# Second feed-forward's chunks in pairs by seven products, unread products at a norm, and the last additions shared out, in a four-layer attention kernel

## The chip, the cores and the metric

The kernel runs on one core of a Trainium2 chip, in float32, from one launch. The metric is the time of the whole launch in microseconds (us); the time of a kernel is the median of its runs. One further execution is taken by the hardware profiler, and all rows of a profile and a trace are of that one. The core's engines have short names in the profile: PE (matrix products), PEld (PE's weight loads, which lie beside the products), DVE (vector), ACT (scalar, with the transcendental functions), POOL (GpSimd) and SP (issues DMAs). L277 is line 277 of the kernel.

## The reference

512 tokens (2 batches of 256) of width 256 pass four layers. Each has a cross-attention to a context of 2 x 512 rows and a feed-forward, both on a layer norm of `x` and added to `x` with a gate:

```python
x = x + jnp.tanh(g_xattn[0]) * _L0_xattn_ref(_layernorm(x), ctx_2048)
x = x + jnp.tanh(g_ffn[0]) * _L0_ffn_ref(_layernorm(x), L0_ffn_W_up, L0_ffn_W_gate, L0_ffn_W_down)
x = x + jnp.tanh(g_xattn[1]) * _L1_xattn_ref(_layernorm(x), ctx_2048, Wq, Wk, Wv, Wo)
x = x + jnp.tanh(g_ffn[1]) * _L1_ffn_ref(_layernorm(x), L1_ffn_w_gate_up, L1_ffn_w_down)
x = x + jnp.tanh(g_xattn[2]) * _L2_xattn_ref(_layernorm(x), ctx_2048, Wq, Wg, bg, Wkv, Wo)
x = x + jnp.tanh(g_ffn[2]) * _L2_ffn_ref(_layernorm(x), router_w, gate_w, up_w, down_w)
x = x + jnp.tanh(g_xattn[3]) * _L3_xattn_ref(_layernorm(x), ctx_2048, mask_BxS2_bk0)
x = x + jnp.tanh(g_ffn[3]) * _L3_ffn_ref(_layernorm(x), router, w_up_gate, w_down, shared_w_up_gate, shared_w_down)
```

The change touches three places of it. The second feed-forward is dense, 256 to 1024 and back:

```python
gate_up = jnp.einsum('bsh,oh->bso', h_shard, w_gate_up)    # 256 -> 2 x 1024
gate, up = jnp.split(gate_up, 2, axis=-1)
h = jax.nn.silu(gate) * up
out = jnp.einsum('bsi,hi->bsh', h, w_down)                 # 1024 -> 256
```

The fourth attention has no weights: softmax of `x` against the context's rows, under a mask, and the same rows as values. The fourth feed-forward takes each token through the two best of eight small experts, `y = sum of w[k] * out_buf[expert k, place k]`, and through one shared expert; both are added.

## The kernel before, in words

**Tiles.** `x` stays in SBUF as four tiles of 128 tokens x 256 (`x[:, n, :]`, NT = 4). A norm takes, for each tile, `bn_stats` and `bn_aggr` on DVE (L217, L218), two POOL instructions for `rstd` (L219 adds epsilon, L220 takes the power -1/2), and one DVE instruction for `xn` (L236, `norm_apply`). Two PE transposes of each tile into PSUM (tag `tr`) and an ACT copy give `xT`, width on the partitions, laid out as batch, half of the width, 256 tokens. Most products with `x` take `xT` as the moving side, 256 columns (one batch) or 512 (both), with two products to a sum, one for each half of the width.

**Who orders the work.** The program is written as one text; for each engine the order of the text is its order, apart from what `inline` does. `inline(i, line)` chains an instruction behind the last one given to the same list: `line` for DVE, `pool_line` for POOL, `pe_line` for PE. Where a list is empty (after `clear()`) no such chain is made and a planner may move the instruction; `None` appended starts a chain anew. `chain` (L277) is the helper that issues nearly all products, so they have one line in the profile; `add_to_x` (L280) is the helper of all additions to `x`, `x = acc * scalar + x` in one DVE instruction. Buffers come from rotating pools: `q4` (4 KB per partition), `q2`, `q1` in SBUF; `ps_mm` (`mm`), `ps_tr` (`tr`, `mm_t`) and `ps_acc` (`acc`) in PSUM. A tile is given out when the earlier user of its buffer is through.

**The second attention**, in front of the first place, has 16 heads of 128. `l1_attend` ends each half head with a reciprocal and a multiplication on DVE and two additions on POOL (`all_t` L840, `all_r` L841), which keep sums for a check of the range. Its keys, queries and values are made in pairs of heads by seven products of blocks: `weight_sums` (L593 on) forms four sums of weight blocks on POOL (L597 to L600), `batch_sums` (L585 on) four sums of the blocks of `xT` (L588 to L591), and `seven_queries` (L651 on) issues seven products of 256 columns and builds four output blocks of 128x256 from them by one ACT copy and four DVE additions (L672, L675, L676, L679). The eight products that the plain way takes are 2 x 2 x 2: two blocks of output columns, two batches, two halves of the width to be summed.

**The second feed-forward** is `dense_ffn`, called once with `whole_keys2` as `between`. Its three weights are `aw`, `lw` (256 x 1024 each) and `dw`. `hidden` (L300 on) goes through eight chunks of 128 columns of the 1024. Chunks 0 and 1 go batch by batch, four products of 256 columns for each batch, and stand between the transposes of the norm and the keys of the third attention (`whole_keys2`, eight tiles of context; `k` is L956), which fill PE while the norm is made. Chunks 2 to 7 take four products of 512 columns each, two for `aw`, two for `lw`; then ACT takes the silu from PSUM and DVE multiplies by the other (L317) into `hT`. `down` then takes one tile of tokens after the other: eight products of 256 columns into `acc`, and `add_to_x`. Behind it comes the third attention's norm. POOL's two DMAs that clear the tables `xg` and `yg` in DRAM, and `iota` and `zero`, stand in the text around it; `k2` and `v2` hold the third attention's keys and values.

**The third feed-forward's end and the fourth attention's norm.** `l2_back` (L1362) puts the experts' rows back to their tokens by products into `y`; `l3_stats` adds `y` to `x` and takes the norm's statistics, `norm_apply` makes `xn`, and `l3_turned(n)` transposes it (L1423). `l3_scores` then takes products of 128 columns against the context into `ps3`, and `l3_exps` the exponentials on ACT.

**The end.** `yg` in DRAM holds each token's two rows; four DMAs gather them to `rows[n]` (`o3g`, L1718 on), two on SP's queue and two on ACT's. `shared_down(n)` gives the shared expert's `accs`. `final(n)` adds a tile's two rows, each times its weight `kept`, by two `add_to_x`; the `accs` take one more. `store(n)` sends the tile out on SP's queue.

Of the kernel before, what the change touches and what calls it, by code (L numbers as in the profile page):

```python
# [17 lines left out]
F32 = mybir.dt.float32  # L18
# [3 lines left out]
AF = mybir.ActivationFunctionType  # L22
# [3 lines left out]
P = 128  # L26
NT = 4
D = 256
T = NT * P
B = 2  # L30
# [19 lines left out]
def flamingo(ctx: ExitStack, tc: tile.TileContext, a: dict, out: bass.AP):  # L50
# [122 lines left out]
    def gf(layer):  # L173
        return tg[:, 4 + layer : 5 + layer]
# [60 lines left out]
    def norm_apply(n, xn, stats):  # L235
        inline(nc.vector.tensor_scalar(xn[:, n, :], x[:, n, :], *stats, ALU.subtract, ALU.mult))  # L236
# [35 lines left out]
    def mm(shape=None):  # L272
        return ps_mm.tile(shape or [P, 512], F32, tag="mm", name="mm")
# [5 lines left out]
    def add_to_x(n, acc, scalar, cols=slice(0, D)):  # L279
        return inline(nc.vector.scalar_tensor_tensor(x[:, n, cols], acc, scalar, x[:, n, cols], ALU.mult, ALU.add))  # L280
# [11 lines left out]
    def load_table(fn, last, why):  # L292

        t = small.tile([P, 1], F32, tag="warm", name="warm", bufs=1)
        behind(nc.scalar.activation(t, eps_ln, fn), last, why)

    def hidden(xT, chunks, act_w, lin_w, hT, both_w=None, pause=lambda ci, b: False):


        ps = {}  # L300
        for ci, (off, sz), ts in by_batch(chunks):
            if sz == 64:
                p = mm()
                chain(p, [(both_w(k), batch(xT, k)) for k in range(2)])
                s = q2.tile([P, T], F32, tag="q2", name="silu")
                nc.scalar.activation(s[64:], p[:64], AF.Silu)
                nc.vector.tensor_mul(hT[ci // 2][64:, ci % 2, :], s[64:], p[64:])
                continue
            if ci not in ps:
                ps[ci] = mm(), mm()  # L310
            pa, pb = ps[ci]
            for w, p in ((act_w, pa), (lin_w, pb)):
                chain(p[:sz, ts], [(w(k, off, sz), batch(xT, k, ts)) for k in range(2)])
            if ts.stop == T:
                s = q2.tile([P, T], F32, tag="q2", name="silu")
                silus[:] = [nc.scalar.activation(s[:sz, :], pa[:sz, :], AF.Silu)]
                nc.vector.tensor_mul(hT[ci // 2][:sz, ci % 2, :], s[:sz, :], pb[:sz, :])  # L317
            if pause(ci, ts.stop // T):
                yield
# [4 lines left out]
    def down(hT, chunks, w, scalar, tiles=range(NT)):  # L324

        for n in tiles:
            acc = ps_acc.tile([P, D], F32, tag="acc", name="acc")
            chain(acc, [(hT[ci // 2][hidden_rows(sz), ci % 2, n * P : (n + 1) * P], w(ci, hidden_rows(sz)))
                        for ci, (_, sz) in enumerate(chunks)])
            add_to_x(n, acc, scalar(n))  # L330
# [262 lines left out]
    def weight_sums(pool, tag, u, v):  # L593

        cols = u.shape[2]
        t = pool.tile([P, 4, cols], F32, tag=tag, name="wsum")
        nc.gpsimd.tensor_add(t[:, 0, :], v[:, 0, :], v[:, 1, :])  # L597
        nc.gpsimd.tensor_sub(t[:, 1, :], t[:, 0, :], u[:, 0, :])
        nc.gpsimd.tensor_sub(t[:, 2, :], u[:, 0, :], v[:, 0, :])
        nc.gpsimd.tensor_sub(t[:, 3, :], u[:, 1, :], t[:, 1, :])  # L600
        return t
# [33 lines left out]
    def seven_keys(p):  # L635
# [8 lines left out]
        def product(dst, w, t):  # L644
# [3 lines left out]
                     context_of(slice(0, M)), product, lambda t: t,  # L648
                     [[t[:, b * M : (b + 1) * M] for b in range(B)] for t in kT])

    def seven_queries(p):  # L651

        w = l1_w[p // 2][0]
        u, v = (w[:, :, (2 * p + i) % 4 * HD : ((2 * p + i) % 4 + 1) * HD] for i in range(2))
        s = weight_sums(q2, "q2", u, v)
        yield
        qT = q4.tile([P, 4, 256], F32, tag="q4", name="qT")
        queries1.append(qT)

        def two(tr, *of):  # L660
            t = ps_tr.tile([P, 2, 256], F32, tag="tr", name="mm_t") if tr else mm([P, 2, 256])
            for i, (w, b) in enumerate(of):
                nc.tensor.matmul(t[:, i, :], lhsT=w, rhs=b, start=True, stop=True)  # L663
            return t

        def both(i):
            return qT[:, i : i + 1, :].to_broadcast([P, 2, 256])

        m1 = two(True, (u[:, 0, :], xT[:, 0, 0, :]))
        nc.scalar.copy(qT[:, 1, :], m1[:, 0, :])  # L670
        m26 = two(False, (u[:, 1, :], xT[:, 0, 1, :]), (s[:, 1, :], x_sums[:, 1, :]))
        nc.vector.tensor_add(qT[:, 0:4:3, :], both(1), m26)  # L672
        yield
        m57 = two(True, (s[:, 0, :], x_sums[:, 0, :]), (s[:, 2, :], x_sums[:, 2, :]))
        nc.vector.tensor_add(qT[:, 1:3, :], both(3), m57)  # L675
        nc.vector.tensor_add(qT[:, 3, :], qT[:, 2, :], m57[:, 0, :])  # L676
        yield
        m34 = two(False, (s[:, 3, :], xT[:, 1, 1, :]), (v[:, 1, :], x_sums[:, 3, :]))
        nc.vector.tensor_add(qT[:, 1:3, :], qT[:, 1:3, :], m34)  # L679
        yield  # L680

    def seven_values(g):

# [23 lines left out]
    def dense_ffn(layer, act, lin, dn, between):  # L707

        aw = act.rearrange("p (k e) -> p k e", k=2)
        lw = lin.rearrange("p (k e) -> p k e", k=2)  # L710
        dw = dn.rearrange("p (c d) -> p c d", d=D)
        pe_line.append(None)
        xn = q4.tile([P, NT, D], F32, tag="q4", name="xn")
        xT = q4.tile([P, B, 2, 256], F32, tag="q4", name="xT")
        hT = [q4.tile([P, 2, T], F32, tag="q4", name="hT") for _ in range(4)]
        chunks = hidden(xT, FCH, lambda k, o, s: aw[:, k, o : o + s], lambda k, o, s: lw[:, k, o : o + s], hT,
                        pause=lambda ci, b: ci < 2)
        for n in range(NT):
            norm_apply(n, xn, norm_stats(n))
            tr = ps_tr.tile([P, 2, P], F32, tag="tr", name="tr")  # L720
            for k in range(2):
                inline(nc.tensor.transpose(tr[:, k, :], xn[:, n, k * P : (k + 1) * P], ident), pe_line)
            nc.scalar.copy(tokens(xT, n), tr)
            if n == 1:
                between(0)
            if n == 2:
                next(chunks)
                between(1)
        for _ in range(3):
            next(chunks)  # L730
        pe_line.clear()
        for _ in chunks:
            pass
        down(hT, FCH, lambda c, s: dw[:, c, :], lambda n: gf(layer))

    def ternary_ffn():

# [204 lines left out]

    half_bg = small.tile([P, 2], F32, tag="half_bg", name="half_bg", bufs=1)
    behind(nc.gpsimd.tensor_scalar_mul(half_bg, bg, 0.5), l0_pool, "its data come late")
    k2 = [q4.tile([P, 4, D], F32, tag="q4", name="k2") for _ in range(B)]
    v2 = [q4.tile([P, 3, 2, P + 1], F32, tag="q4", name="v2") for _ in range(3)]
    for t in v2:
        nc.gpsimd.memset(t[:, :, :, P : P + 1], 1.0)
    def negatives(z):
        t = q2.tile(list(z.shape), F32, tag="q2", name="fm")  # L950
        inline(nc.vector.tensor_scalar_min(t, z, 0.0))
# [34 lines left out]


    load_table(AF.Exp, silus[0], "the table of exponentials with tanh")
    kv = q2.tile([P, B, 2, P], F32, tag="q2", name="kv")
    ks = small.tile([P, B, 2, 8], F32, tag="ks2", name="ks2", bufs=1)  # L990
    for t in (line, pe_line):
# [378 lines left out]
    for q in range(QUADS + 2):  # L1370
# [15 lines left out]
            hTs[q] = l2_turn(h)  # L1386
        if q >= 2:
            l2_back(q - 2, os.pop(q - 2), backs.pop(q - 2), y)
    pe_line.clear()
    shd = slab[:, 0, 0 : 6 * D].rearrange("p (c d) -> p c d", d=D)  # L1390
    nc.gpsimd.memset(shd[0:64, 5, :], 0.0)
    nc.sync.dma_start(shd[:, 0:5, :], a["l3_shd"][0 : 5 * P, :].rearrange("(c p) d -> p c d", p=P))
# [13 lines left out]
    nc.vector.reduce_sum(none, p, axis=AX.X)  # L1406
    nc.vector.tensor_scalar(none, none, 0.0, None, ALU.is_le)

    for t in (line, pe_line):
        t.append(None)  # L1410
    xn = q4.tile([P, NT, D], F32, tag="q4", name="xn")
    xT = q4.tile([P, B, 2, 256], F32, tag="q4", name="xT")
    ctxT_rows3 = ctxT.rearrange("p b k (h i r) -> p b k h i r", h=2, r=2)
# [6 lines left out]
    def l3_turned(n):  # L1420
        tr = ps_tr.tile([P, 2, P], F32, tag="tr", name="tr")
        for k in range(2):
            inline(nc.tensor.transpose(tr[:, k, :], xn[:, n, k * P : (k + 1) * P], ident), pe_line)  # L1423
        nc.scalar.copy(tokens(xT, n), tr)
# [44 lines left out]
    l3_stats(3)  # L1469
    norm_apply(2, xn, stats3[2])  # L1470
    norm_apply(3, xn, stats3[3])
    l3_turned(0)
    l3_scores(0, ps3[0], slice(0, P), [0])
    l3_turned(1)
# [140 lines left out]
    def shared_down(n):  # L1615
        acc = ps_acc.tile([P, D], F32, tag="acc", name="acc")
        chain(acc, [(hS[c // 2][:, c % 2, n * P : (n + 1) * P], shd[:, c, :]) for c in range(6)])
        return acc
# [104 lines left out]
    def final(n):  # L1723
        for k in range(2):
            add_to_x(n, rows[n][:, k, :], kept[:, k, n : n + 1])

    def store(n):
        nc.sync.dma_start(out[n * P : (n + 1) * P, :], x[:, n, :])

    for n in range(2):  # L1730
        add_to_x(n, accs[n], gf(3))
    accs = [shared_down(n) for n in (2, 3)]
    final(0)
    store(0)
    add_to_x(2, accs[0], gf(3))
    for n in (1, 2):
        final(n)
        store(n)
    final(3)
    add_to_x(3, accs[1], gf(3))  # L1740
    store(3)
    line.clear()
    pe_line.clear()
    return nc.values_load(bad[0:1, 0:1], min_val=0, max_val=1, skip_runtime_bounds_check_because="a comparison's result is 0 or 1")
# [654 lines left out]
```

## Time and profile before

| what | us |
|---|---|
| three timed runs | 579.69, 580.5, 583.82 (median 580.5) |
| the profiled execution | 582.43 |
| its span (first to last instruction) | 580.7 |
| PE, PEld busy | 557.2, 396.8 |
| DVE, ACT, POOL busy | 357.1, 176.8, 202.1 |
| second feed-forward's last unbroken stretch of products | 357.53 to 396.5 |
| first transpose of the fourth attention's norm | 489.71 |
| rows of the four tiles gathered (tiles 0 to 3) | 571.6, 571.2, 572.9, 572.4 |
| last DVE addition ends | 576.37 |

How to read the lines that the prediction shows. A line of the page's first part gives an engine's busy time, its share of the span and, behind an x, its instructions. The chain of waits follows the work that ended last back from the end, each step to what released it; a line of it has the start in us, the time that it adds, the engine, what it is (PE steps by the name of the tile written) and the line, and "issue" is time in which an engine waited for nothing that the profile shows. A group of instructions has engine, line, operation, tile written, tiles read and shape; `x68` is their number; in a list of single instructions the numbers are start and duration, and behind them in brackets the idle time in front and what ended it. A product of two float32 matrices is recorded as two PE instructions. A line of the windows gives a stretch of time, its length, the busy time of PE, PEld, DVE, ACT and POOL with the number of instructions, the mean granted clock of PE (1 is full speed), and the DMA engines' share and rate.

### The profile page before, as it was taken

What the parts mean: (1) busy time and instruction counts of PE and PEld (TensorE: products, weight loads), DVE (VectorE), ACT (ScalarE), POOL (GpSimd) and SP (SyncE); (2) the same over time, 40 slices, a digit from 0 to 9 for tenths busy, and PEclk for the clock granted to TensorE, in tenths of its full rate; (3) what the DMA queues carried; (4) which work ended last, traced back from release to release, by engine and by line L of the source; (5) the groups of instructions that cost most, each with busy time, mean ns of one, the idle gap of its engine ahead of it and who ended that gap; (6) DMA issues with size and microseconds to landing.
All of it is one profiled execution on the core that took longest, in us unless ns stands there. A gap on an engine that the chain in (4) does not pass through costs nothing.

```text
span 580.7 us, 8632 instructions
## 1 busy us (share of the span) xinstructions
PE 557.2 (96%) x3254; PEld 396.8 (68%) x3254; DVE 357.1 (61%) x722; ACT 176.8 (30%) x351; POOL 202.1 (35%) x338
## 2 busy tenths in 40 slices
PE   8989999999999999999999999999999998999994
PEld 6554675778788787878787786477675446884453
DVE  5898444687857887588867984124567336462323
ACT  5874543422212222122213213112313211432210
POOL 3787456535333464134343332011020002151240
PEclk9999999999999999999999999999989998899998
DMA  7905200002002200202041447042021999313013
GB/s 292 408 12 196 94 0 1 0 2 73 1 0 74 72 2 0 73 0 73 0 146 72 147 144 227 9 144 74 0 73 62 378 413 369 98 46 115 17 43 122
DMA packets 15528, 59.14 MB, mean 102 GB/s; under 512 B 2654, under 2 KB 5925, under 8 KB 11847
## 3 DMA queue, kind: packets, MB, share of 16 engines
q1 hardware_dynamic: 13430, 53.70, 25.2%
q0 software_dynamic: 1472, 4.28, 2.3%
q8 instruction: 27, 0.44, 0.3%
q10 hardware_dynamic: 576, 0.53, 0.3%
q14 instruction: 23, 0.18, 0.1%
HBM read 53.70 MB, written 5.25 MB: 102 GB/s over the span
## 4 chain that ended last, share of the span: by engine, by line
PE 85%; DVE 8%; DMA 2%; issue 1%; ACT 1%; POOL 1%; SPq 0%; POOLq 0%; DVEq 0%; ACTq 0%
PE mm L277 29%; PE acc L277 20%; PE mm_t L645 4%; PE mm L1317 4%; PE mm_t L691 4%; PE mm L645 3%; PE mm L691 3%; PE s L450 2%; PE mm L1645 2%; PE mm L663 2%; PE acc L1338 2%; PE mm_t L663 2%; PE acc L462 2%; DVE x L280 1%; PE outT L758 1%
## 5 line engine op out<-in xcount | busy, mean ns | idle before, releaser
L819 ACT ACTIVATE e<-mm 128x512 f32<-128x512 f32 x64 | 38.0, 597 | 115.1 <-PE mm L277 112.6
L838 DVE RECIPROCAL r<-acc 128x256 f32<-128x256 f32 x32 | 56.2, 1757 | 20.4 <-PE acc L277 20.3
L277 PE MATMUL mm<-qT,kT 128*128 128x256 f32 x256 | 61.1, 380 | 0.0
L277 PE MATMUL acc<-e,slab 128*128 128x256 f32 x256 | 60.5, 379 | 0.0
L277 PE MATMUL mm<-xT,slab 128*128 128x256 f32 (+1 forms) x180 | 59.0, 481 | 0.8 <-DVE k L956 0.8
L277 PEld LDWEIGHTS acc<-e,slab 128*128 128x128 f32 x256 | 48.6, 190 | 9.2 <-issue 2.9
L277 PEld LDWEIGHTS mm<-qT,kT 128*128 128x128 f32 x256 | 47.7, 190 | 9.4 <-issue 2.9
L840 POOL TENSOR_TENSOR all_t<-all_t,t 128x256 f32<-128x256 f32 x32 | 24.1, 753 | 80.8 <-DVE t L824 80.8
L277 PEld LDWEIGHTS mm<-xT,slab 128*128 128x128 f32 x180 | 33.4, 190 | 22.0 <-issue 18.2
L841 POOL TENSOR_TENSOR all_r<-all_r,r 128x256 f32<-128x256 f32 x32 | 23.3, 728 | 57.5 <-DVE r L838 57.5
L219 POOL TENSOR_TENSOR rstd<-mv,eps_ln 128x1 f32<-128x1 f32 x26 | 6.4, 246 | 96.3 <-DVE mv L218 96.3
L454 ACT ACTIVATE e<-s 128x512 f32<-128x512 f32 x64 | 32.8, 606 | 7.6 <-PE s L450 7.5
L823 DVE TENSOR_TENSOR t<-e,e 128x512 f32<-128x512 f32 x32 | 22.9, 716 | 15.2 <-ACT e L819 14.7
L280 DVE SCALAR_TENSOR_TENSOR x<-acc,tg,x 128x256 f32<-128x256 f32 x28 | 13.5, 482 | 26.7 <-PE acc L277 26.6
L277 PE MATMUL acc<-slab,oT 128*128 128x256 f32 x128 | 29.1, 381 | 0.4 <-DVE oT L839 0.4
L277 PE MATMUL mm<-slab,ctxT 128*128 128x512 f32 x64 | 29.0, 594 | 0.0
L277 PEld LDWEIGHTS acc<-slab,oT 128*128 128x128 f32 x128 | 23.7, 190 | 4.4 <-DVE oT L839 1.2
L829 ACT CAST th<-t 128x256 fp32r<-128x256 f32 x28 | 11.3, 405 | 45.5 <-DVE t L827 45.5
L1317 PE MATMUL mm<-slab,xsT 128*32 128x512 f32 x192 | 22.7, 596 | 0.2 <-ACT xsT L1272 0.2
L830 POOL TENSOR_TENSOR th<-t 128x256 fp32r<-128x256 f32 x28 | 20.5, 732 | 5.5 <-DVE t L827 4.9
L450 PE MATMUL s<-slab,ctx_nat 32*128 32x256 f32 x256 | 20.8, 401 | 1.0 <-DMA ctx_nat<-in_ctx 1.0
L1551 POOL DMA_INDIRECT yg<-o,xg_sb x10 | 9.7, 973 | 30.7 <-DVE o L187 24.4
(389 smaller groups left out, 1105.1 us busy)
## 6 DMA issues: line engine op xcount, KB each, us to landing
slab<-in_l_gu_all SPq DMA_DIRECT2D x16, 1024.0 KB, 4.9
slab<-in_l_all SPq DMA_DIRECT2D x4, 2048.0 KB, 10.6
slab<-in_l_dn_all SPq DMA_DIRECT2D x4, 1024.0 KB, 5.9
slab<-in_l_dn_all SPq DMA_DIRECT2D x8, 512.0 KB, 10.1
slab<-in_l_gu SPq DMA_DIRECT2D x4, 704.0 KB, 11.6
ctx_nat<-in_ctx SPq DMA_DIRECT2D x4, 512.0 KB, 8.9
slab<-in_l_up SPq DMA_DIRECT2D x2, 1024.0 KB
slab<-in_l_gate SPq DMA_DIRECT2D x2, 1024.0 KB, 11.1
```

Source lines behind the costliest of these rows:

```text
L277: inline(nc.tensor.matmul(dst, lhsT=lhsT, rhs=rhs, start=(i == 0), stop=(i == len(pairs) - 1)), pe_line)
L450: in_turn(nc.tensor.matmul(ps[j][:, k, :], lhsT=ctx_nat[rows, b, hf, c * P : (c + 1) * P], rhs=qm[rows, n, i, :], start=True, stop=True))
L454: exps.append(nc.scalar.activation(es[j], ps[j], AF.Exp))
L645: nc.tensor.matmul(dst, lhsT=w, rhs=t, start=True, stop=True)
L663: nc.tensor.matmul(t[:, i, :], lhsT=w, rhs=b, start=True, stop=True)
L691: nc.tensor.matmul(dst[:, j, :], lhsT=t[:, j * P : (j + 1) * P], rhs=w, start=True, stop=True)
L819: nc.scalar.activation(e, s, AF.Exp, scale=HD ** -0.5)
L823: nc.vector.tensor_add(t, es[0], es[1])
L838: nc.vector.reciprocal(r, acc[:, 1, :])
L840: nc.gpsimd.tensor_add(all_t, all_t, t)
L841: nc.gpsimd.tensor_add(all_r, all_r, r)
L1317: inline(nc.tensor.matmul(ps[j * BLK : (j + 1) * BLK, :], lhsT=xsT[k][:, (4 * q + j) * BLK : (4 * q + j + 1) * BLK], rhs=gu2[:, home(q, j) ...
```

## The change

Three things are changed.

**The second feed-forward.** Chunks 0 and 1 stay with `hidden`. Chunks 2 to 7 go in three pairs: for each pair and each of `aw` and `lw`, `weight_sums` forms four sums (the first pair's are in the text ahead of the norm), and `seven_blocks`, which is the body of `seven_queries` under a name of its own, makes the pair's two chunks for both batches by seven products of 256 columns. The blocks of `aw` are written to `hT`, those of `lw` to a new tile `lin`; then, for each chunk, ACT takes the silu of `hT` in place and DVE multiplies it by `lin`. `batch_sums` forms the sums of `xT`. The way down takes chunks 0 to 5 of tiles 0 and 1, then chunks 6 and 7 of both, then tile 2, then tile 3. `k2` and `v2` are given out in two steps.

**The fourth attention's norm.** `l2_back`'s last product is kept as the head of `pe_line`, and behind it, ahead of the first transpose, stand three products of the identity with `ctxT` of 512, 512 and 128 columns into a buffer of `ps3`, which nothing reads before `l3_scores` writes it anew.

**The end.** For tiles 2 and 3 ACT multiplies the two rows by their weights and POOL adds them (`final_apart`); DVE adds the sum in one operation. The order of the additions and stores is written anew.

In the compiled program this gives PE 42 products of 256 columns in place of 24 of 512, and the three unread ones; the first of the 42 stands among the second batch's first products of the chunks 0 and 1. On POOL the eight weight sums of the first pair stand between the last two additions to `all_r` (L841) and ahead of the norm's `rstd` (L219, L220), and `zero` and the two DMAs that clear `yg` and `xg` stand behind all weight sums. SP's order is as it was.

```diff
+    def seven_blocks(out, u, v, s, xT, x_sums):
...
+        m1 = two(True, (u[:, 0, :], xT[:, 0, 0, :]))
+        nc.scalar.copy(out[:, 1, :], m1[:, 0, :])
+        m26 = two(False, (u[:, 1, :], xT[:, 0, 1, :]), (s[:, 1, :], x_sums[:, 1, :]))
+        nc.vector.tensor_add(out[:, 0:4:3, :], both(1), m26)
+        yield
+        m57 = two(True, (s[:, 0, :], x_sums[:, 0, :]), (s[:, 2, :], x_sums[:, 2, :]))
+        nc.vector.tensor_add(out[:, 1:3, :], both(3), m57)
+        nc.vector.tensor_add(out[:, 3, :], out[:, 2, :], m57[:, 0, :])
+        yield
+        m34 = two(False, (s[:, 3, :], xT[:, 1, 1, :]), (v[:, 1, :], x_sums[:, 3, :]))
+        nc.vector.tensor_add(out[:, 1:3, :], out[:, 1:3, :], m34)
+        yield
...
+        yield from seven_blocks(qT, u, v, s, xT, x_sums)
...
+        def pair_of(w, c):
+            u, v = (w[:, :, (c + i) * P : (c + i + 1) * P] for i in range(2))
+            return u, v, weight_sums(q2, "q2", u, v)
+
+        pairs = [(pair_of(aw, 2), pair_of(lw, 2))]
+        chunks = hidden(xT, FCH[:2], lambda k, o, s: aw[:, k, o : o + s], lambda k, o, s: lw[:, k, o : o + s], hT,
...
+        sums = q4.tile([P, 4, 256], F32, tag="q4", name="x_sums")
+        batch_sums(sums, xT)
         for _ in chunks:
             pass
-        down(hT, FCH, lambda c, s: dw[:, c, :], lambda n: gf(layer))
+        for c in (2, 4, 6):
+            if c < 6:
+                pairs.append((pair_of(aw, c + 2), pair_of(lw, c + 2)))
+            lin = q4.tile([P, 4, 256], F32, tag="q4", name="lin")
+            h = hT[c // 2]
+            for out, of in zip((h.rearrange("p c (b t) -> p (c b) t", b=B), lin), pairs.pop(0)):
+                for _ in seven_blocks(out, *of, xT, sums):
+                    pass
+            for i in range(2):
+                silus[:] = [nc.scalar.activation(h[:, i, :], h[:, i, :], AF.Silu)]
+                nc.vector.tensor_mul(h[:, i, :], h[:, i, :], lin[:, 2 * i : 2 * i + 2, :].rearrange("p b t -> p (b t)"))
+
+        accs = {}
+        for tiles, parts in (((0, 1), (range(6), range(6, 8))), ((2,), (range(8),)), ((3,), (range(8),))):
+            for part in parts:
+                for n in tiles:
+                    if n not in accs:
+                        accs[n] = ps_acc.tile([P, D], F32, tag="acc", name="acc")
+                    for c in part:
+                        nc.tensor.matmul(accs[n], lhsT=hT[c // 2][:, c % 2, n * P : (n + 1) * P], rhs=dw[:, c, :],
+                                         start=(c == 0), stop=(c == 7))
+            for n in tiles:
+                add_to_x(n, accs[n], gf(layer))
...
+    for cols in (512, 512, 128):
+        inline(nc.tensor.matmul(ps3[1][1].rearrange("p r q -> p (r q)")[:, 0:cols], lhsT=ident, rhs=ctxT[:, 0, 0, 0:cols],
+                                start=True, stop=True), pe_line)
     l3_turned(0)
...
+    def final_apart(n):
+
+        for k in range(2):
+            nc.scalar.mul(rows[n][:, k, :], rows[n][:, k, :], kept[:, k, n : n + 1])
+        nc.gpsimd.tensor_add(rows[n][:, 0, :], rows[n][:, 0, :], rows[n][:, 1, :])
+
...
     accs = [shared_down(n) for n in (2, 3)]
+    for n in (2, 3):
+        final_apart(n)
     final(0)
     store(0)
     add_to_x(2, accs[0], gf(3))
-    for n in (1, 2):
-        final(n)
+    final(1)
+    store(1)
+    for n in (2, 3):
+        if n == 3:
+            add_to_x(3, accs[1], gf(3))
+        inline(nc.vector.tensor_add(x[:, n, :], x[:, n, :], rows[n][:, 0, :]))
         store(n)
-    final(3)
-    add_to_x(3, accs[1], gf(3))
-    store(3)
```

## The prediction

> **What bounds the kernel now.** I read the page's first two parts, then the chain that ended last, then three stretches of it in order of time. PE is the bound: 96% busy, and 85% of the chain.
>
> ```profile
> PE 557.2 (96%) x3254; PEld 396.8 (68%) x3254; DVE 357.1 (61%) x722; ACT 176.8 (30%) x351; POOL 202.1 (35%) x338
> ...
> PE 85%; DVE 8%; DMA 2%; issue 1%; ACT 1%; POOL 1%; SPq 0%; POOLq 0%; DVEq 0%; ACTq 0%
> ```
>
> So an edit counts where it shortens PE's stream or one of the few stretches in which PE waits. The change touches three. The first is the second feed-forward. The chain there is PE without a break from 357.53 to 396.5, after a wait of 0.80 us for `k` (L956):
>
> ```profile
> 357.05 0.43 DVE k L956
> 357.49 0.04 issue
> 357.53 25.18 PE mm L277 x68
> 382.71 13.81 PE acc L277 x64
> ```
>
> An f32 product is two matmul records. A 256-column record costs 13.81/64 = 0.216 us, so a 256-column product 0.432. Of the 68 records 20 have 256 columns (4.32 us); the other 48, the 24 products of chunks 2 to 7, take 20.86.
>
> The second is the fourth attention's norm, and here the reader must look at the clock beside the idle time (columns: stretch, length, PE, PEld, DVE, ACT, POOL busy, clock, DMA):
>
> ```profile
> 487.00:489.00 2.00, 0.46 (x4) 0.26 (x3) 1.87 (x5) 0.00 (x0) 0.65 (x2) 1.00 1.02 414
> 489.00:491.00 2.00, 0.83 (x3) 0.46 (x4) 1.90 (x8) 0.37 (x1) 1.22 (x4) 0.68 1.06 328
> 491.00:493.00 2.00, 2.00 (x10) 2.00 (x11) 1.24 (x4) 0.00 (x0) 1.37 (x3) 0.50 1.08 205
> 493.00:495.00 2.00, 2.00 (x11) 2.00 (x10) 0.41 (x1) 1.62 (x2) 0.00 (x0) 0.50 0.84 222
> 495.00:497.00 2.00, 2.00 (x14) 2.00 (x13) 0.00 (x0) 0.29 (x2) 0.00 (x0) 0.61 0.69 213
> ```
>
> PE runs out of work at 487.46 and gets the first transpose at 489.71 (idle 2.24); then the granted clock is 0.5 for 6.83 us, until about 496.6, though PE is busy.
>
> The third is the end: one DVE chain of ten 0.48 us additions, from the landing of the first gathered rows to the last store.
>
> ```profile
> 571.64 1.01 DVE L280 SCALAR_TENSOR_TENSOR x<-o3g,kept,x 128x256 f32<-128x256 f32 x2 [3.63 <-DMA o3g<-yg]
> 572.56 0.48 DVE L280 SCALAR_TENSOR_TENSOR x<-acc,tg,x 128x256 f32<-128x256 f32 x1
> 572.96 2.83 DVE L280 SCALAR_TENSOR_TENSOR x<-o3g,kept,x 128x256 f32<-128x256 f32 x6
> 575.89 0.48 DVE L280 SCALAR_TENSOR_TENSOR x<-acc,tg,x 128x256 f32<-128x256 f32 x1
> ```
>
> **Part 1, chunks in pairs.** *PE.* The 24 products of 512 columns (20.86 us) become 3 pairs x 2 weights x 7 = 42 of 256 columns, 18.13 us: 2.73 less. The new order puts the first of the 42 (`mm_t`, needing only turned tiles) between chunk 1's products of the first batch, in the 0.80 us wait for `k`; 0.43 more is hidden, 3.16 in all.
>
> *POOL in front.* The weight sums of pair 1, eight additions of 128x128, stand on POOL between the last two additions to `all_r` (L841), and the second norm's `rstd` (L219, L220) stands behind them. POOL is free for them at 342.57; L597 to L600 with these shapes take 0.457 us and start 0.41 apart, about 3.2 us. Then `all_r` (0.67 to the next start) and the first `rstd` at 346.45 instead of:
>
> ```profile
> 345.50 0.19 POOL L219 TENSOR_TENSOR rstd<-mv,eps_ln 128x1 f32<-128x1 f32 x1 [0.76 <-DVE mv L218]
> ...
> 353.63 0.41 DVE L236 TENSOR_SCALAR xn<-x,mv,rstd 128x256 f32<-128x256 f32 x1 [0.94 <-POOL rstd L220]
> ```
>
> DVE holds `xn` in order, so all four tiles come 0.95 later (the fourth at 354.6). PE follows: its third transpose, at 351.82 right behind the `xn` of 351.21, waits, and `k` comes at 358.5 instead of 357.5. I charge the whole 0.95; bounds 0 (PE has keys' products to go between) and 1.3 (eight full 0.457).
>
> *POOL behind.* The sums of `xT` (four additions of 0.72, rows of L588 to L591) can start when the last `xT` is copied, 357.4, and are done by 361; PE asks at 363.3. The other 16 weight sums are 2 or more us ahead of PE. The two DMAs that clear `yg` and `xg` (1.20 and 0.98 us on POOL) move behind all these, to about 368; their tables are first written at 514. Cost nothing.
>
> *DVE and ACT.* A pair needs, for each weight, one ACT copy (0.37), three additions of 512 and one of 256 elements, all of which the second attention's queries show:
>
> ```profile
> L672 DVE TENSOR_TENSOR qT<-qT,mm x7: 675/681/689, 119.3 to 307.9; 128x512 f32<-128x512 f32 x7
> L675 DVE TENSOR_TENSOR qT<-qT,mm_t x7: 628/679/682, 125.9 to 311.1; 128x512 f32<-128x512 f32 x7
> L676 DVE TENSOR_TENSOR qT<-qT,mm_t x7: 410/420/421, 126.6 to 312.0; 128x256 f32<-128x256 f32 x7
> ```
>
> That is 2 x (3 x 0.68 + 0.42) + 2 multiplications of 0.69 = 6.3, with gaps of 0.03 about 6.6 us a pair, against 14 x 0.432 = 6.04 on PE. DVE is the slower by 0.6 a pair. It starts at 364 (behind chunk 0's and 1's multiplications) and ends at 383.8. PE, starting the other 41 products at 358.5 + 4.32 = 362.8, ends at 380.5. What covers the lag is the split way down: tiles 0 and 1 first take chunks 0 to 5, 12 products or 5.2 us, so chunks 6 and 7 are asked for at 385.7. Margin 1.9. Without the split tile 0 would ask at 383.1 and PE wait 0.7. The buffers that PE gets back from DVE come 0.8 us or more ahead of need.
>
> *Down* keeps its 64 records: 380.5 + 13.8 = 394.3 instead of 396.5. Tile 0's addition comes later within the stage, the last tile's does not, and that starts the next norm. **Part 1: -2.2 us.**
>
> **Part 2, unread products.** Two f32 products of 512 and one of 128 columns: 0.86 + 0.86 + 0.22 = 1.94 us, in line behind the last product into `y` and ahead of the first transpose: 487.1 to 489.0. The transpose needs `xn`, there at 489.6, so they delay nothing; their buffer has been read long before. Idle falls from 2.24 to about 0.7 us. If the clock stays at 1: transpose at 489.71, copy, scores from 490.6; a 128-column record at full clock is (4.41 - 16 x 0.216)/8 = 0.12 by the stretch from 497.14, so 24 records take 2.9 and three turns 0.66, and the point that PE passed at 497.14 comes at 494.1. The exponentials (0.42 each, table loaded by 493.4) keep up. Everything behind hangs on this PE stream; the weights for it have landed by 502, at 100 to 200 GB/s for the last 6 us, and the first is needed at 508. **-3.0 us**; bounds 0 and -3.2.
>
> The Trainium skill, "TensorE: Matmul & The Clock Gate", section "Why this matters for your kernels", asks only for no PE gaps over about 3 us. By that a gap of 2.24 would be harmless and part 2 worth nothing; the rows above disagree, the clock being at 0.5 behind it. The same page ("What's actually happening") has a free-running window of 3.413 us; the trace agrees with that, its half-clock stretches lasting 3.413 (near 430) and 6.827 us.
>
> **Part 3, the end.** Tiles 2 and 3 get their two weighted rows on ACT (2 x 0.42) and their sum on POOL (0.73); DVE does eight operations instead of ten. Rows land at 571.6 (tile 0), 571.2 (1), 572.9 (2), 572.4 (3). ACT takes tile 2 first: 573.8; POOL 574.6; DVE, free at 574.0 after tile 1, waits, adds (0.40) to 575.05 and the last down product to 575.5. ACT ends tile 3 at 574.65, POOL at 575.45, DVE at 575.9 instead of 576.37: -0.45. Against it: DVE's addition and POOL's overlap, both reading two tiles of SBUF. In such an overlap at 330.68 the addition of L823 took 1.04 instead of 0.69. Then POOL's second sum waits for DVE, and the gain is -0.1. I take **-0.2**.
>
> The Trainium skill, "SBUF — State Buffer", section "Who interferes with whom", says that one blocks the other for the whole instruction; the rows near 330.68 agree roughly (0.35 lost in 0.49 of overlap), and by the rule part 3 is worth the 0.1.
>
> **Sum.** -2.2 - 3.0 - 0.2 = -5.4 us. The profiled execution took 582.43 (span 580.7, 1.7 around it), so 577.0 by its own account. The median shown is 580.5, 1.9 below the profiled one; the same difference gives **575.1 us**, 0.9% faster.
>
> **Rivals.** (a) *The products buy little in the timed runs.* The profiled run lies 1.9 above the median: half-clock stretches fall where a free window happens to lie, and the timed runs may not have had the one at 490. Against: the gap's neighbours (idle again 490.4 to 490.8) leave few positions that escape. Then -2.4: 578.1. Chance 0.25. (b) *More than forecast*: the front delay is swallowed by keys' products (0.95) and the end gives 0.45, or the stretch near 430 falls elsewhere: 573.5. Chance 0.14. (c) *DVE becomes the pair loop's bound*: at 0.8 us an addition of 512, pairs take 7.5 and end at 386.5; with waits on buffers part 1 falls to about -1: 576.5. Chance 0.07. (d) *Slower*, by the same place at a higher price: POOL's weight sums hold up DVE's additions. Three pairs must end at 391 before the 5.4 is gone, 9.0 us a pair, so 0.98 for each of the eight large operations; over 1% slower needs 1.22. For it: L823's 1.04. Against: the additions read PSUM and only one SBUF tile, and POOL is done by 368. 590 at the worst. Chance 0.04. The forecast has 0.50.
>
> The 1% that a measurement can tell is 5.8 us, 574.7 here. Forecast and (b) lie below it for about 0.37; slower by over 1% 0.04; the rest, 0.59, within. The range leaves out the ends of (a) and (b), and of (a) less than of (b), since the front delay may reach its 1.3 and the end give nothing: 572.5 to 580.0.
>
> **What would show it.** PE's products of the pairs in a row without idle, from 363 to 380.5; first `rstd` of the second norm near 346.4; `acc` from 380.5 without a wait for `hT`; clock 1.00 from 487 to 500 and scores' 128-column records at 0.12; the last addition near 576 less what came before. Wrong if the clock falls despite the products, if PE waits for DVE in the pairs, or if the norm's delay exceeds 1.3.

## The result

| | before | changed |
|---|---|---|
| median of 13 runs each | 580.64 us (577.69 to 584.19) | 577.78 us (575.65 to 579.79) |
| ratio, 95% interval | | 0.9941 (0.9920 to 0.9963) |
| profiled execution, its span | 582.43, 580.7 us | 578.43, 576.6 us |
| mean granted clock of the profiled execution | 0.986 | 0.991 |

The ratio is 3.4 us or 0.6%, where the forecast had 5.4. The spans of the two profiled executions differ by 4.1 us. Where these lie is read from the changed kernel's trace by the same views as before.

The page's first part and its chain of waits by engine: PE has 42 records more and 0.7 us less to do, and is the bound as it was.

```profile
PE 556.5 (97%) x3296; PEld 403.3 (70%) x3296; DVE 370.5 (64%) x744; ACT 180.7 (31%) x361; POOL 216.4 (38%) x368
...
PE 85%; DVE 7%; POOL 2%; issue 1%; ACT 1%; DMA 1%; another core or an unknown queue 1%; SPq 0%; POOLq 0%; DVEq 0%; ACTq 0%
```

The chain in the second feed-forward (start, us, what; the changed kernel's lines are numbered anew, L657 is in `seven_blocks`, L765 the way down):

```profile
344.84 0.41 POOL wsum L600
345.25 0.68 POOL all_r L875
345.93 0.16 POOL rstd L219
...
357.37 0.43 DVE k L997
357.80 0.04 issue
357.84 4.58 PE mm L277 x20
362.43 0.86 PE mm L657 x4
...
379.26 0.86 PE mm L657 x4
380.13 13.81 PE acc L765 x64
```

The pairs' products run from 362.43 to 380.13 without a gap. The chain now goes through POOL's weight sums to the norm. The two executions are 0.42 us apart at the first product with the context (7.73 us before, 7.31 here) and 0.62 at the end of the second attention, ahead of the change, so the stage is timed from the last reciprocal of the second attention (342.10 before, 341.48 here): the first `rstd` comes 1.01 us later after it (4.40 instead of 3.39), `k` ends 0.94 later (16.31 instead of 15.37), the way down begins 1.97 earlier (38.48 instead of 40.45), and ends as much earlier.

The fourth attention's norm, with the clock in the column behind POOL:

```profile
487.00:489.00 2.00, 1.70 (x7) 0.77 (x5) 1.90 (x7) 0.00 (x0) 1.39 (x4) 1.00 1.06 414
489.00:491.00 2.00, 1.54 (x13) 1.46 (x13) 1.90 (x7) 0.37 (x1) 1.02 (x3) 1.00 1.08 199
491.00:493.00 2.00, 2.00 (x19) 2.00 (x19) 0.68 (x2) 1.76 (x3) 0.82 (x2) 1.00 1.06 228
493.00:495.00 2.00, 2.00 (x16) 1.92 (x15) 0.00 (x0) 2.00 (x6) 0.00 (x0) 1.00 0.86 197
495.00:497.00 2.00, 2.00 (x11) 1.82 (x10) 1.12 (x2) 0.95 (x3) 0.00 (x0) 1.00 0.70 169
```

The clock stays at 1.00. From the start of the last product into `y` to the first product of the softmax's denominators (`den`) it was 14.20 us and is 11.38: 2.82 less.

But between the two, in the third feed-forward's routing, half clock has come where it wasn't before (first the kernel before, then the changed one):

```profile
432.00:435.00 3.00, 2.76 (x12) 1.85 (x11) 2.38 (x7) 0.00 (x0) 1.01 (x3) 1.00 0.00 0
435.00:438.00 3.00, 2.35 (x15) 1.88 (x16) 0.82 (x3) 1.43 (x5) 1.97 (x3) 1.00 0.00 0
```

```profile
432.00:435.00 3.00, 2.11 (x13) 1.35 (x12) 1.24 (x5) 1.35 (x4) 1.99 (x4) 1.00 0.00 0
435.00:438.00 3.00, 3.00 (x13) 2.19 (x13) 1.48 (x8) 1.68 (x3) 0.24 (x1) 0.74 0.01 3
```

From the start of the way down's last product to the first product into `y` it was 64.53 us, with one stretch of 3.413 us at half clock (428.3), and is 66.13 with two (426.2 and 436.4): 1.60 lost in code that the change doesn't touch.

The end, DVE's additions in order of time:

```profile
567.39 1.01 DVE L280 SCALAR_TENSOR_TENSOR x<-o3g,kept,x 128x256 f32<-128x256 f32 x2 [3.19 <-DMA o3g<-yg]
...
570.39 0.43 DVE L1797 TENSOR_TENSOR x<-x,o3g 128x256 f32<-128x256 f32 x1 [0.68 <-POOL o3g L1779]
570.73 0.48 DVE L280 SCALAR_TENSOR_TENSOR x<-acc,tg,x 128x256 f32<-128x256 f32 x1
571.44 0.42 DVE L1797 TENSOR_TENSOR x<-x,o3g 128x256 f32<-128x256 f32 x1 [0.22 <-POOL o3g L1779]
```

From the first addition's start to the last one's end: 4.47 us instead of 4.74. So the profiled difference is -0.62 (start, not the change) - 1.97 (pairs) + 1.60 (half clock at 436) - 2.82 (half clock at 490 gone) - 0.27 (end), -4.08 of the 4.1 us. Two further differences cancel: from `den` to the addition of the first gathered rows it takes 69.86 us instead of 70.25, and from the last addition to the span's end 4.79 instead of 4.36. The rows settle what part 1 does in its stage and that DVE's last addition comes earlier. What is open is the clock: whether its half stretches belong to the change or to the execution, and what part 2 is then worth in the timed runs.

**A count for the clock.** The profile's busy time of PE doesn't tell a thin stretch: a product of 8 columns is recorded with 0.25 us, though at the rate of the large ones its columns take 0.007. So I counted columns: each PE record streams for 0.843 ns a column from its start (from 0.2158 us for 256), at most until the next record starts, twice as long and half as much at half clock; summed over windows of 3.413 us on the grid on which the clock changes. In the trace of before the window from 424.9 has 0.28 and that from 486.3 0.32, and both are followed by half clock. In that of the changed kernel 422.8 (0.37) and 433.0 (0.26). The grid lies elsewhere in each execution, so a thin place can be hit or missed by its position.

### The profile page after: what moved, and what is told of

Its sections match the earlier page's. It is cut to its first block, busy times and chain, and to the rows that moved or that the text cites. A ratio compares the mean times of both kernels' runs of the same rounds, so it can differ in the third digit from the quotient of the medians.

```text
span 576.6 us, 8805 instructions
## 1 busy us (share of the span) xinstructions
PE 556.5 (97%) x3296; PEld 403.3 (70%) x3296; DVE 370.5 (64%) x744; ACT 180.7 (31%) x361; POOL 216.4 (38%) x368
## 4 chain that ended last, share of the span: by engine, by line
PE 85%; DVE 7%; POOL 2%; issue 1%; ACT 1%; DMA 1%; another core or an unknown queue 1%; SPq 0%; POOLq 0%; DVEq 0%; ACTq 0%
PE mm L277 25%; PE acc L277 17%; PE mm_t L645 4%; PE mm L657 4%; PE mm L1361 4%; PE mm_t L695 4%; PE mm L645 3%; PE mm_t L657 3%; PE mm L695 3%; PE acc L765 2%; PE s L450 2%; PE mm L1693 2%; PE acc L1382 2%; PE acc L462 2%; PE outT L792 1%
## 5 line engine op out<-in xcount | busy, mean ns | idle before, releaser
L277 PE MATMUL mm<-xT,slab 128*128 128x256 f32 (+1 forms) x132 | 38.4, 441 | 0.3 <-DVE k L997 0.3
L219 POOL TENSOR_TENSOR rstd<-mv,eps_ln 128x1 f32<-128x1 f32 x26 | 6.3, 243 | 69.3 <-DVE mv L218 69.2
L277 PEld LDWEIGHTS mm<-xT,slab 128*128 128x128 f32 x132 | 24.3, 190 | 10.4 <-issue 7.2
```

Of the source, the lines that this page charges most:

```text
L277: inline(nc.tensor.matmul(dst, lhsT=lhsT, rhs=rhs, start=(i == 0), stop=(i == len(pairs) - 1)), pe_line)
```

## The experiments

All times are medians. Each set ran on one chip, the three sets on three. The kernel before took 577.97, 578.38 and 578.69 us in the three sets below and 580.64 in the first comparison, so only ratios and kernels of one set are compared. (The two traces of the first comparison take 69.9 and 70.3 us from `den` to the first gathered rows, the twelve others 68.3 to 69.0; why isn't known.) "Clock" is the mean granted clock, averaged over the runs.

### Each part alone, and the weight sums behind the norm

Parts 1, 2 and 3 were put alone into the kernel before. For the fourth kernel, the first pair's sums of the changed one were moved behind the norm's four `rstd`:

```diff
-        pairs = [(pair_of(aw, 2), pair_of(lw, 2))]
         chunks = hidden(xT, FCH[:2], ...
...
+        pairs = [(pair_of(aw, 2), pair_of(lw, 2))]
         for _ in range(3):
             next(chunks)
```

Expected of part 1 alone:

> The kernel before with part 1 alone (pairs by seven products, way down in parts). My theory: the stage gives what its own trace shows, PE's stream shorter by 2.9 us less 0.95 us of front delay, so -2.0 us: 578.6 us against 580.6; in the trace the first rstd of the second norm about 1.0 us later after the last but one reciprocal than before, and the way down ending 2.0 us earlier after it. Rival (the missing gain is eaten by part 1 itself, by what it moved out of the stage): the stage ends 2.0 us earlier but the whole only 0.6, 580.0 us, and the loss shows in every run, at full clock.

Expected of part 2 alone:

> The kernel before with part 2 alone (three unread products). My theory: windows of 3.413 us that lie anywhere; in the trace of before each window that begins between about 486.0 and 488.9 has PE streaming less than 0.4 of it, so 2.9 of 3.4 positions cost about 2.9 us: -2.5 us on the average, 578.1 us, and the granted clock of its runs higher than that of before by some 0.004. Rival (the forecast's (a), the timed runs seldom had that stretch): 580.2 us and the same clocks. By the Trainium skill's rule of gaps up to 3 us (TensorE: Matmul & The Clock Gate, Why this matters for your kernels) the gap of 2.24 us costs nothing: 580.6 us.

Expected of part 3 alone:

> The kernel before with part 3 alone (the end shared out). Forecast: -0.2 us, 580.4 us. By the trace of the changed kernel the last DVE addition comes 0.26 us earlier after the first (4.47 instead of 4.73 us), but the last store ends 0.23 later after it: 0.0 us in the time, 580.6 us. Rival (POOL's sums and DVE's additions block each other): the second POOL sum takes 1.2 us or more and the last addition comes no earlier, 580.8 us.

Expected of the sums behind the norm:

> The changed kernel with the first pair's eight weight sums behind the second norm's four rstd on POOL. My theory: the sums held up the norm by 1.0 us and nothing hid it; without them k comes 0.9 us earlier, the sums are still in time (done by 361, asked for at 362), and the time is 576.9 us, 0.9 below the changed kernel's 577.8. Rival (the keys' products swallow the delay): within 0.2 us of the changed kernel. Rival (the sums now come too late): PE waits for wsum at the pairs' second product and the time is 578 us or more.

| kernel | us | ratio to before (95%) | clock (before 0.9928) |
|---|---|---|---|
| part 1 alone | 577.24 | 0.9985 (0.9961 to 1.0009) | 0.9912 |
| part 2 alone | 577.49 | 0.9981 (0.9960 to 1.0001) | 0.9958 |
| part 3 alone | 577.54 | 0.9997 (0.9980 to 1.0014) | 0.9942 |
| changed, sums behind the norm | 574.68 | 0.9940 (0.9922 to 0.9958) | 0.9958 |

*Part 1 alone* is undecided by its ratio: the interval holds 0.6 us as well as 2.0. In its trace the stage is the same to about 0.01 us as in the changed kernel (`rstd` 4.41, `k` 16.31, way down 38.48 after the last reciprocal). Its runs had less clock than those of before, and runs picked by equal clock tell more: at 0.995 it took 575.27, 575.64 and 575.92 us, the kernel before at the same clock between 576.7 and 578.4, most near 577.7. That is the 2.0 of the stage; a steadier measure follows below.

*Part 2 alone* raises the clock by 0.003, and by the runs' means gains 1.2 us (577.27 against 578.48), half of what I expected; the interval of its ratio reaches from a gain of 2.3 us to none. The trace of part 3 alone shows why. It has the old gap, and the clock falls in it, but for one window (columns as above):

```profile
485.00:487.00 2.00, 0.10 (x1) 0.00 (x0) 1.86 (x7) 0.00 (x0) 0.79 (x3) 1.00 0.99 403
487.00:489.00 2.00, 1.19 (x5) 0.92 (x6) 1.90 (x7) 0.37 (x1) 1.37 (x4) 0.64 1.07 307
489.00:491.00 2.00, 2.00 (x12) 2.00 (x11) 1.26 (x4) 0.18 (x1) 1.05 (x3) 0.51 1.10 219
491.00:493.00 2.00, 2.00 (x19) 2.00 (x19) 0.06 (x1) 1.64 (x3) 0.00 (x0) 1.00 0.78 212
```

From the last product into `y` to `den` this took 12.65 us: 1.27 more than 11.38, not 2.82. And in the trace of part 1 alone, again with the old gap, the windows lie so that none falls, and it takes 11.38. So the gap costs 2.82, 1.27 or nothing, by position; I had priced each position that hits at the dearest.

*Part 3 alone* shows no gain: its ratio, 0.9997, has an interval from 1.2 us less to 0.8 more. Its trace has DVE's last addition 4.47 us after the first one's start, as in the changed kernel. But the span ends 4.77 us behind that addition. In the nine traces with the new end this stretch is 4.45 to 4.91 us, 4.76 in the mean, and in the five with the old end 4.34 to 4.62, 4.46 in the mean: 0.30 more, as much as the addition comes earlier.

*The sums behind the norm* do what was expected in the trace. First POOL's first `rstd`, in order of time; then the chain:

```profile
345.47 0.19 POOL L219 TENSOR_TENSOR rstd<-mv,eps_ln 128x1 f32<-128x1 f32 x1 [0.76 <-DVE mv L218]
```

```profile
357.03 0.43 DVE k L997
357.46 0.04 issue
357.50 4.58 PE mm L277 x20
...
379.79 13.81 PE acc L765 x64
```

With its last reciprocal at 342.08, `rstd` is back at 3.39 and `k` at 15.37 behind it, and the way down begins at 37.55, 0.94 earlier than in the changed kernel; the sums, from 353.53 on, are in time. The 0.95 of the forecast is a real price and could be saved; a timed comparison within one set follows below.

### More and fewer unread products

If thin windows bring half clock, more columns in the two thin places of the routing must end it, and fewer at the fourth norm must bring it back. The first kernel adds to the changed one:

```diff
     place = ps_acc.tile([P, NT, E], F32, tag="acc", name="acc")
+    p = ps_tr.tile([P, 512], F32, tag="tr", name="tr")
+    inline(nc.tensor.matmul(p[:, 0:384], lhsT=ident, rhs=iota[:, 0:384], start=True, stop=True), pe_line)
     places(place, near_r, hot, halves[0])
...
     busy(384)
+    busy(96)
...
-    for fn in turned:
-        fn()
+    turned[0]()
+    busy(256)
+    turned[1]()
```

(`busy(cols)` is the kernel's own helper for such a product; three stood there before. Counted with the first, this makes three more, not four as the expectations say.) The second has these and the weight sums behind the norm. The third is the changed kernel without them, with `for cols in (512,)` in place of `(512, 512, 128)`.

> The changed kernel itself, beside the same runs of the kernel before as the three below. My theory: its timed runs differ by which of three gaps (begin of window 421.9 to 422.9, 431.7 to 434.0, and none left at 487) meet a window of the clock; ratio to before 0.994 again, 3.4 us less. Rival (the parts measured alone add up, 0.15 + 0.19 + 0.03%): 0.996, 2.1 us less.

> The changed kernel with four more unread products in the two gaps left: 384 columns ahead of the routing's second places (L1170), 96 more and 256 more around the later transposes (L1142). My theory: a window in which PE streams less than about 0.4 is followed by one of half clock; the thinnest windows rise from 0.31 to 0.50 and from 0.33 to 0.52, no stretch of half clock is left between 420 and 500, the granted clock is 0.998 in nearly every run, and the median is 1.5 us below that of the changed kernel, the spread of its runs under 2 us. Rival (only the length of a gap counts, and gaps here are under 1 us already): clocks as in the changed kernel, and 0.3 us more for products that stand in the way.

> The products of the run above and the weight sums behind the rstd together. My theory: both gains add, 0.9 and 1.5 us: 2.4 us below the changed kernel, 5.8 below the kernel before. Rival: the earlier norm shifts the gaps against nothing that is fixed, so the sums' gain shows only if the clock's windows are no longer met by chance; if more unread products do nothing, 0.9 below the changed kernel.

> The changed kernel with one unread product of 512 columns at the fourth attention's norm instead of three. My theory: the window there has 0.60 of streaming with three and 0.28 with one (1.08 us less of 3.41), under 0.4 for two of three positions, which cost 2.8 us each: 1.8 us above the changed kernel on the average, clocks lower by 0.003. Rival (one product breaks the gap into two short ones, and that is enough): the same as the changed kernel.

| kernel | us (lowest to highest) | ratio to before (95%) | clock (before 0.9918) |
|---|---|---|---|
| changed | 575.19 (574.25 to 576.94) | 0.9931 (0.9905 to 0.9958) | 0.9962 |
| with more unread products | 574.17 (573.85 to 574.68) | 0.9919 (0.9894 to 0.9943) | 0.9973 |
| and the sums behind the norm | 573.39 (572.89 to 573.62) | 0.9904 (0.9879 to 0.9928) | 0.9977 |
| one unread product of 512 | 576.42 (574.18 to 577.68) | 0.9962 (0.9941 to 0.9982) | 0.9938 |

At the first thin place of the changed kernel a slice is filled like this, and these are two groups of its products, with 8 and 128 columns each:

```profile
423.00:426.00 3.00, 2.53 (x17) 2.02 (x18) 1.73 (x10) 0.62 (x1) 0.00 (x0) 1.00 0.00 0
...
423.40 1.03 PE L277 MATMUL den<-ks,qry 128*128 128x8 f32 x8
...
425.80 0.79 PE L1088 MATMUL tr<-ident,wide_r 128*128 128x128 f32 x4 [0.41 <-ACT wide_r L1076]
```

The windows of the first kernel, at the two places where the changed kernel had stretches at half clock:

```profile
423.00:426.00 3.00, 2.59 (x17) 2.08 (x17) 1.73 (x9) 0.62 (x1) 0.00 (x0) 1.00 0.05 19
426.00:429.00 3.00, 3.00 (x17) 2.63 (x17) 2.40 (x8) 0.00 (x0) 0.00 (x0) 1.00 0.00 0
...
432.00:435.00 3.00, 2.93 (x19) 2.25 (x19) 0.94 (x6) 2.03 (x5) 1.42 (x2) 1.00 0.00 0
435.00:438.00 3.00, 3.00 (x14) 2.25 (x15) 2.51 (x10) 0.64 (x2) 0.00 (x0) 1.00 0.01 3
```

PE is as busy by the profile as before in 423 to 426 (2.59 of 3.00 against 2.53 in the changed kernel) and its longest idle time is the same 0.41 us, but there are more columns in the window (0.48 of it streaming), and the clock stays. From the way down's last product to `y` it takes 63.03 us; without a half stretch and without the products (part 2 alone, part 3 alone) it took 62.91 and 62.94, so they stand in the way for 0.1 us, and each half stretch there costs 1.6 (64.52 with one, 66.02 to 66.13 with two). The spread of the runs shrinks from 2.7 to 0.8 us, so most of what was left of it was the clock. The median falls by 1.0, not by the 1.5 expected; the changed kernel's own runs seem to have hit the places less often in this set than I had counted (their mean clock is 0.9962, in the first comparison 0.9936). With the sums behind the norm it falls by another 0.78. This kernel takes 573.39 us, 1.0% less than before, and is the best of the study. One unread product in place of three costs 1.2 us and 0.0024 of clock (expected 1.8 and 0.003). That breaking the gap in two isn't enough rests on these timed runs, whose ranges overlap; the one trace, of the fastest run, has no half stretch at the norm.

Taken together, and apart from each launch's start and end, the fourteen traces have ten windows that are followed by half clock, with 0.25, 0.26, 0.26, 0.27, 0.28, 0.32, 0.32, 0.35, 0.37 and 0.37 of their time streaming. The thinnest that are not so followed have 0.33, 0.35, and then 0.38 and more. My count is a model (it knows starts, not streams), so the border is somewhere at a third.

The place at 431 to 437 brought half clock in four of the five traces that have the pairs and no product added there (not in that with one unread product), and in none of the three without the pairs. That could make part 1 guilty of it. The timed runs speak against it: part 2 alone and the changed kernel with the sums behind the norm, without and with the pairs, have the same mean clock, 0.9958.

### The other parts at a steady clock

With the thin places filled, the runs of a kernel lie within 0.5 to 1.3 us. The last set has the filled kernel and three others, all with the three more unread products: without the pairs (the kernel before with all unread products and the old end), without the new end, and with the way down tile by tile:

```diff
-        for tiles, parts in (((0, 1), (range(6), range(6, 8))), ((2,), (range(8),)), ((3,), (range(8),))):
+        for tiles, parts in (((n,), (range(8),)) for n in range(NT)):
```

> The kernel before with all the unread products (the three of the change and the four more), without the pairs and with the old end: the clock is full in nearly all its runs, so what the pairs are worth shows against the next kernel free of it. My theory: part 1 is worth the 1.97 us of its stage's trace, this is 576.2 us when the one with the pairs is 574.2, and the spread of its runs is under 2 us. Rival (part 1's gain is lost again behind its stage): within 0.8 us of the one with the pairs. The forecast's figure was 2.2.

> The changed kernel with the four more unread products and with the old end. My theory: part 3 is worth 0.1 (DVE's last addition 0.27 earlier after its first, the span's tail up to 0.2 longer): 0.1 us above the full one. The forecast's figure was 0.2 and the bounds 0.1 and 0.45.

> The changed kernel with the four more unread products, and the way down tile by tile, each with all eight chunks. The forecast: PE waits 0.7 us at tile 0 for the last product of DVE. By the trace of the changed kernel DVE ends chunk 7 at 383.13 and tile 0 would ask at 383.15: a wait of 0.1 or none, the same time as the full one within 0.2.

> The changed kernel with the four more unread products once more, as the measure for the three above: 574.2 us, spread under 2 us, ratio to before 0.992.

| kernel | us (lowest to highest) | ratio to before (95%) |
|---|---|---|
| no pairs, old end | 576.60 (576.31 to 577.09) | 0.9957 (0.9939 to 0.9974) |
| pairs, old end | 574.57 (573.73 to 575.04) | 0.9921 (0.9895 to 0.9948) |
| pairs, new end, way down by tiles | 574.47 (574.20 to 574.69) | 0.9918 (0.9892 to 0.9944) |
| pairs, new end, way down in parts | 574.39 (573.76 to 574.67) | 0.9914 (0.9888 to 0.9940) |

Part 1 is worth 576.60 - 574.57 = 2.03 us, the 1.97 of its stage, and the runs of the two kernels don't overlap: nothing of it is lost behind. For part 3 the medians differ by 0.18 (0.19 by the means); within a spread of about 1 us over six runs that can't be told from nothing. Nor can the 0.08 of the split; in the chain it is, first of the kernel by tiles, then of that in parts, worth 0.30:

```profile
380.35 14.11 PE acc L765 x64
```

```profile
380.74 13.81 PE acc L765 x64
```

## Why the prediction was right, and where it was not

The direction and the range held; 577.2 to 577.8 lies well inside 572.5 to 580.0. The 5.4 us of the forecast were 3.4, and the rival (a), 578.1, is nearer than the forecast, 575.1.

**Part 1, forecast 2.2, measured 1.97 in the stage and 2.03 in time: right.** The delay of the norm by POOL was charged at 0.95 and is 1.01 at the `rstd` and 0.94 at `k`; that nothing swallows it was a choice, and the run with the sums behind the norm confirms it, and so does the 0.78 us of the same edit in the filled kernel. The 41 products take 17.70 us, 0.432 each, as worked out. The 0.2 too much is in the term that was removed: of the 25.18 us of the 68 records I took off 4.32 for the first twenty, while twenty take 4.58 when they start from a standstill, as the changed kernel's chain shows; the other 48 were 20.60, not 20.86. DVE didn't hold up PE: it took 6.58 us a pair (forecast 6.6), began at 363.40, 0.6 earlier than forecast, and ended the last pair at 383.13 instead of 383.8. So the split covers a wait of 0.30, not 0.7.

**Part 2, forecast 3.0: the mechanism right, the term mis-sized for the timed runs.** In the profiled executions the stage became 2.82 shorter, near the 3.0. The step that failed is the last one of the sum: the whole difference was set against the profiled execution and then carried to the median with a constant 1.9. The 1.9 was itself the clock, as far as the runs show: the profiled execution had its windows at the dearest position, where 6.83 us go at half clock, and a mean clock of 0.986. In the first set of runs the kernel before took 581.3 to 581.9 us at 0.985 and 577.8 in the mean of the 21 of 33 runs at 0.993 to 0.996. The traces show three prices of the gap, 2.82, 1.27 and nothing, and its removal was worth 1.2 us by the means of the timed runs, less than half of the term, with an interval from nothing to 2.3. Rival (a) named this, with the argument against it that few positions escape. Both happened: in the trace of part 1 alone the gap escaped, and in that of part 3 alone one window fell instead of two.

**The stretch at 436: not in the forecast.** I looked for thin stretches where the change adds products and took the rest of the kernel as fixed. The place at 431 to 437 was in the trace of before (a window of 0.35 that just got by); that kernels meet it by chance, with or without the pairs, fits the clocks of the timed runs and isn't proved. In the profiled execution of the changed kernel it cost 1.60 and hid part of the gain.

**Part 3, forecast 0.2 between 0.1 and 0.45: right for DVE, not shown in time.** DVE's last addition comes 0.27 earlier. What stands behind it was put at no change, and is 0.30 longer in the traces; why stays open. In time nothing is clear of noise (0.18 in the last set, 0.0003 of the ratio alone). ACT's rows took 0.49 each, not 0.42, and POOL's second sum 0.98 instead of 0.73, as DVE's addition from 570.39 overlapped it; that addition took its usual 0.43. The Trainium skill, "SBUF — State Buffer", section "Who interferes with whom", has whoever issues first keep the shared ports for the whole instruction and the other wait; the trace agrees in who waits, but POOL lost 0.25 for an overlap of about 0.4, less than the whole of it.

Part 1, at a steady clock, and part 2, by the means of its own runs, add up to 2.0 + 1.2 = 3.2 us; the two comparisons of the changed kernel gave 3.4 and 4.0. The total leans on how often the windows fell badly in each set, so where it lies in the range is in part luck.

The rivals (c) and (d) are out: DVE's large additions took 0.68 to 0.69, as in the second attention, and POOL's weight sums didn't lengthen them.

## What to carry to other kernels

Before a profiled difference is carried to the timed runs, look in both traces for stretches at half clock: if they lie in different places, part of the difference belongs to the execution, and the change should be priced at full clock and the clock apart. Thin places are found by counting columns, not by PE's busy time or the length of gaps, and unread products of a few hundred columns in waits that are there anyway cost 0.1 us here and made the kernel both faster and steadier (runs within 0.8 us instead of 2.7). A helper's work moved to an idle engine still stands in that engine's order: look at what is queued behind it, as the eight weight sums ahead of the norm show (0.94 us).

## What the runs showed of the hardware

The clock falls to half for one window of 3.413 us after a window in which PE streams columns for less than about a third of the time (all of 0.32 or less, none of 0.38 or more, in fourteen traces, by the count above), though in the slice around such a window the profile has PE busy for 84% (2.53 of 3.00 us) with no idle time longer than 0.41 us. The Trainium skill, "TensorE: Matmul & The Clock Gate", section "Why this matters for your kernels", warns of idle gaps of PE over about 3 us between bursts of products; here the gap of 2.24 us at the fourth norm was enough for 6.83 us at half clock, and many small products between idle times of 0.2 to 0.4 us for 3.413. A half window costs 1.27 to 1.6 us here, and a second one followed twice, each time behind a window at half clock that was itself thin (0.37 from 489.7 in the kernel before, 0.26 from 434.0 in the repeated changed kernel).
